# Starting a weight quantisation earlier and spacing it differently, beside a cross-attention on one core

## The chip, the cores and the metric

The kernel runs as one program on one core of a Trainium2 chip. The core has five instruction queues: PE (TensorE, matmuls), DVE (VectorE), ACT (ScalarE), POOL (GpSimd) and SP (SyncE, which here only issues transfers). Each queue runs its instructions in the order in which they were written; they meet through semaphores. The metric is the device time of one execution in microseconds (us).

## The reference, cut to what matters

A layer of a Perceiver-like network, in float32: 16 batches of 64 latents (1024 rows of width 512), each with a context of 512 rows of width 512.

```
x = x + cross_attention(latents = layernorm(x), context)    # 16 batches, 8 heads of 64
x = x + differential_self_attention(layernorm(x))            # rope, two softmaxes, rms norm
x = x + fp4_feed_forward(layernorm(x))

def cross_attention(latents, context):        # per batch
    kv = concat(norm(context), norm(latents)) @ w_kv          # keys and values, 512 + 64 rows
    out = softmax(q @ k.T) @ v
    return norm(out @ w_out) * g_o + b_o

def fp4_quant_dequant(w):                      # blocks of 16 along the last dimension
    scale = max(max(|block|) / 6, 1e-12)
    return grid_round(w / scale) * scale       # to 0, 0.5, 1, 1.5, 2, 3, 4, 6 with the sign

def fp4_feed_forward(x):                       # w_gate, w_up: 1408 x 512, w_down: 512 x 1408
    h = silu(q(x) @ q(w_gate).T) * (q(x) @ q(w_up).T)
    return q(h) @ q(w_down).T
```

The three weights of the feed-forward part are quantised on the chip, too. That work depends on nothing but the weights.

## The kernel before

Every float32 product is made of three products of rounded float32 (fp32r) halves: high by high, high by low, low by high. "High" is a copy into fp32r (on ACT), "low" the difference (on DVE or POOL). A product of 128 x 512 with a contraction of 512 is 12 matmuls.

The program has four stages: the latents' queries, keys and values (`latents`); the cross-attention, a loop over the 16 context batches (`cross_attention`, L1199); the self-attention over 8 tiles of 128 latent rows (`att.rest`); the feed-forward part (`ff.rest`). Up to the end of the self-attention each engine runs in the order in which the Python code writes its instructions (`in_order`, L87); so where a helper is called in the loop decides what it stands behind on every engine.

One context batch `b` of the loop, as PE sees it: four key products (`keys`, PSUM tile `pk`), the scores of the first two head groups (`scores(b, 0)`, `sim`), the weighting with the probabilities of the batch before (`finish(b - 1)`, `av`), the scores of the second two (`scores(b, 1)`), then four value products (`values`, `pv`) with the transpose of the latents' probabilities (`turn_latents`, `prlt`) after the second of them. The product tiles share three PSUM buffers (`ps_mm`), the scores two (`ps_sim`). DVE scales the keys (L953, `k<-pk,row`), makes the masked minimum of the softmax (L1000, `least`), takes context statistics (L329, L330) and half of the low halves of the next context (L376, `x<-raw,x`; the other half is POOL's). ACT makes the exponentials (L1004), scales the values (L966), copies the high halves (L370) and splits and joins the probabilities for a transposing transfer (`halves` L1040, `join` L1060).

Every second batch finishes a tile `p` of 128 latent rows. For it, odd batches from 3 on (`done` is set) hold the output product as well: `out_turn`, `out_low`, `out_product(p)` (PSUM tile `po`), then `out_norm(p)` (L1155: DVE writes `oz`), then `out_add(p)` (L1161: three passes on POOL, the last of which adds to `x`). The next even batch takes the moments of the new `x` (`out_moments`, `st_a` on DVE at L150, then POOL).

Into this loop the quantisation of the feed-forward weights is laced. `Quantise` holds 35 jobs, pieces of 128 x 512 or 128 x 384. The loop calls `tick()` at up to ten places per batch, the steps; at a step each active piece advances by one yield, and every fourth step starts a new piece. A piece takes ten steps: a load issued by POOL (L287, `qw`), two steps on a reduce group on DVE (L199 to L203), then POOL's multiply with the reciprocal (L205), then a mask on DVE (L208) and a Relu on ACT (L211), two steps later two DVE passes (L213, L214), POOL's multiply with the scale (L216), DVE's 32 x 32 transpose (L296) and ACT's high copy (L297) into `qhl`, and DVE's subtraction (L299) with a store to DRAM issued by POOL (L301). `qw` has three buffers, `qe` and `qhl` one each. In batch 0 the step at the end of the loop body is the only one; batch 1 has eight, the others ten. POOL also makes the low halves of the output weight (`weight_o`, L135, `wol`) at the end of batch 0.

`moments` (L145) makes a tile's mean and 1/sqrt(var + eps) with two DVE instructions and two small POOL ones; `shift` (L162) adds a third POOL one, the negative product of the two, so that `shifted` (L169) can normalise with one ACT instruction.

Of the kernel before, what the change touches and what calls it, by code (L numbers as in the profile page):

```python
# [9 lines left out]
F32 = mybir.dt.float32  # L10
# [10 lines left out]
P = 128  # L21
# [225 lines left out]
class Quantise:  # L247
# [3 lines left out]

    EVERY = 4

    def __init__(self, cm, sc, i):
        self.cm, self.sc = cm, sc
        self.jobs = []
        for c, (at, n) in enumerate(CHUNKS):
            for w, name in (("g", "w_gate"), ("u", "w_up")):  # L260
                self.jobs += [(w, c, k, i[name][k * P : (k + 1) * P, at : at + n]) for k in range(KC)]
        for c, (at, n) in enumerate(CHUNKS):
            self.jobs += [
                ("d", c, k, i["w_down"][at + k * P : at + (k + 1) * P, :]) for k in range(n // P)
            ]
        self.jobs.reverse()
        self.clock, self.active = 0, []

    def home(self, w1, w2):
        self.w1, self.w2 = w1, w2  # L270

    def tick(self, new=True):

        if new and self.jobs and self.clock % self.EVERY == 0:
            self.active.append(self.piece(*self.jobs.pop()))
        self.clock += 1
        self.active = [job for job in self.active if next(job, None)]

    def finish(self, all=False):
# [589 lines left out]
def cross_attention(tc, cm, sc, i, cw, cx, w1, w2, att, quant):  # L869
# [21 lines left out]
    def columns_of(r):  # L891

        first = S * (1 - r)
        return slice(first, first + N + S), slice(S - first, S - first + N)

    state = {}
# [25 lines left out]
    def mask(b):  # L922
        if b < B:
            nc.scalar.activation(
                masks[b % 2][:, S : S + N], state[b]["mu"], AF.Identity, bias=cm.masked, scale=MASKED
            )
# [17 lines left out]
    def keys(b, m):  # L944

        k = ends[b, m // 2][:, m % 2, :]
        hi, lo = cx.done[b]
        cols = slice(m * P, (m + 1) * P)
        ps = cm.mm(f"pk_{b}_{m}")
        cm.product(  # L950
            ps, lambda c: (w_k[0][:, c, cols], w_k[1][:, c, cols], hi[:, c, :], lo[:, c, :]), range(KC)
        )
        nc.vector.tensor_tensor(k[:, S : S + N], ps, cx.row[b], ALU.mult)  # L953
        state[b]["k"].append(k)
# [14 lines left out]
    def scores(b, a):  # L969

        st = state[b]
        st["sim", a] = pss = [cm.two(f"sim_{b}_{a}_{r}") for r in range(2)]
        for h in range(2):
            for r in range(2):
                rows = slice(r * S, (r + 1) * S)
                at = columns_of(r)[0].start + h * half
                for c in range(2):
                    m = 2 * a + c
                    nc.tensor.matmul(  # L979
                        pss[r][c * S : (c + 1) * S, h, :half],  # L980
                        lhsT=queries[b % 2][rows, m, :],
                        rhs=st["k"][m][rows, at : at + half],
                        start=True,
                        stop=True,
                    )

    def softmax(b, a):
        st = state[b]
        both = w1.tile([P, 2 * (N + S)], F32, tag="pr", bufs=2, name=f"pr_{b}_{a}")
        st["whole", a] = both  # L990
        st["pr", a] = both.rearrange("p (r n) -> p r n", r=2)

        def two(t):
            return t.rearrange("p (h n) -> p h n", h=2)

        for r, ps in enumerate(st.pop(("sim", a))):
            mask = masks[b % 2][:, columns_of(r)[0]]
            pr = st["pr", a][:, r, :]
            least = cm.small.tile([P, 1], F32, tag="least", name=f"least_{b}_{a}_{r}")
            nc.vector.tensor_tensor_reduce(  # L1000
                two(pr), ps[:, :, :half], two(mask), -1.0, BIG, ALU.add, ALU.min, least
            )
            t = 2 * a + r
            nc.scalar.activation(  # L1004
                pr, pr, AF.Exp, bias=least, scale=-1.0, accum_out=st["tot"][:, t : t + 1]
            )
# [121 lines left out]
    def out_turn(p):  # L1128
        o = state.pop(("o", p))
        pt = cm.tr(f"ot_{p}")  # L1130
        cm.transpose_chunks(pt, o.rearrange("p a c r d -> p (a c r d)"), KC)
        oh = w1.tile([P, KC, P], F32R, tag="oh", name=f"oh_{p}")
        ol = w2.tile([P, KC, P], F32R, tag="ol", name=f"ol_{p}")
        for k in range(KC):
            src, bias = pt[:, k * P : (k + 1) * P], cw.bv[:, k : k + 1]
            nc.scalar.activation(oh[:, k, :], src, AF.Identity, bias=bias)
        state["oT", p] = oh, ol, pt
# [9 lines left out]
    def out_product(p):  # L1147
        oh, ol, _ = state.pop(("oT", p))
        po = cm.mm(f"po_{p}")
        cm.product(  # L1150
            po, lambda k: (oh[:, k, :], ol[:, k, :], w_o[0][:, k, :], w_o[1][:, k, :]), range(KC)
        )
        state["po", p] = po, cm.moments(po, f"o_{p}")

    def out_norm(p):  # L1155
        po, mv = state.pop(("po", p))
        z = w2.tile([P, D], F32, tag="one", name=f"oz_{p}")
        cm.normalize(z, po, f"o_{p}", mv)
        state["oz", p] = z

    def out_add(p):  # L1161
# [5 lines left out]
    def out_moments(p):  # L1167
        cm.shift(cm.x[p], f"a_{p}", cm.x_mv[:, p, :])
# [29 lines left out]
    cx.load(2)  # L1198
    for b in range(B):  # L1199

        def tick():
            if b:
                quant.tick()

        done = (b - 3) // 2 if b >= 3 and b % 2 else None
        last = b == B - 1
        keys(b, 0)
        if b:
            cx.load(b + 2)
        if last:  # L1210
            att.load("Wq")
            att.load("Wk")
        cx.high(b + 1, 0)
        if b >= 4 and b % 2 == 0:
            out_moments((b - 4) // 2)
        if b > 1:
            tick()
        if done is not None:
            out_turn(done)
        keys(b, 1)  # L1220
        cx.low(b + 1, 0)
        cx.high(b + 1, 1)
        if b:
            join(b - 1, 0)
        if b > 1:
            tick()
        keys(b, 2)
        if b:
            mask(b)
        if done is not None:  # L1230
            out_low(done)
        cx.fetch(b + 2, 0)
        if b == 0:
            for k in range(KC):
                load_o(k)
        cx.flat(b + 1)
        cx.low(b + 1, 1)
        cx.high(b + 1, 2)
        if b:
            join(b - 1, 1)  # L1240
        tick()
        if last:
            att.split("Wq", 0, 1)
        if b == 0:
            scores(b, 0)
            softmax(b, 0)
        keys(b, 3)
        cx.fetch(b + 2, 1)
        if b:
            scores(b, 0)  # L1250
            softmax(b, 0)
        cx.low(b + 1, 2)
        cx.high(b + 1, 3)
        if b:
            finish(b - 1)
            scores(b, 1)
            softmax(b, 1)
            around(b + 1, 1)
            around(b + 2, 0)
        tick()  # L1260
        values(b, 0)
        if b and not last:
            halves(b, 0)
        cx.every(b + 1)
        cx.low(b + 1, 3)
        cx.stats(b + 2, 0)
        tick()
        if last:
            att.split("Wq", 2, 3)
            att.load("Wv")  # L1270
        if b == 0:
            scores(b, 1)
            softmax(b, 1)
            around(b + 1, 1)
            around(b + 2, 0)
        values(b, 1)
        if b == 0:
            halves(b, 0)
        if not last:
            turn_latents(b)  # L1280
            halves(b, 1)
            send(b, 0)
        begin(b + 1)
        latents_values(b + 1)
        cx.fetch(b + 2, 2)
        cx.stats(b + 2, 1)
        tick()
        if last:
            att.norm(0)
            att.split("Wk", 0, 1)  # L1290
        tick()
        if done is not None:
            out_product(done)
        tick()
        values(b, 2)
        if not last:
            send(b, 1)
        cx.fetch(b + 2, 3)
        cx.stats(b + 2, 2)
        tick()  # L1300
        if done is not None:
            out_norm(done)
            out_add(done)
        if b == 0:
            weight_o(0)
            weight_o(1)
        if b == 5:
            att.sa.work()
        if last:
            att.split("Wk", 2, 3)  # L1310
            att.load("Wo")
            att.turn(0)
        values(b, 3)
        cx.stats(b + 2, 3)
        cx.spread(b + 2)
        if b == 0:
            weight_o(2)
            weight_o(3)
        quant.tick()
# [693 lines left out]
```

## Time and profile before

| | |
|---|---|
| median of 3 runs | 876.33 us (874.78 to 876.99) |
| the profiled execution | 878.15 us, span 876.4 us |
| busy in the span: PE, DVE, ACT, POOL | 98%, 79%, 56%, 39% |
| transfers | 126.79 MB, mean 145 GB/s |
| first key product of batch 0, last of batch 15 | 81.6 us, 529 us |
| mean granted TensorE clock | 0.996 of full speed |

All times of a view count from the start of the span. "Busy" is time in which an engine's datapath ran; matmuls are pipelined, so a row for several of them shows the stretch that they span. In a list of waits, `A <- B` says that engine A sat idle before an instruction until B had ended; the numbers are the total, the count and the longest. In the order of time a bracket at the end of a row gives the idle time before it and what ended it. In a table of stretches, the columns are the stretch, its length, the busy time of each engine with the number of instructions, the granted clock, the share of the 16 DMA engines and the rate.

### The profile page before, as it was taken

How to read it: one execution, taken by the hardware profiler on the slowest of the kernel's cores; microseconds unless marked ns; L12 is line 12 of the kernel's file. 1: busy time of each engine (PE TensorE's matmuls, PEld its weight loads, DVE VectorE, ACT ScalarE, POOL GpSimd, SP SyncE). 2: the span in 40 equal slices, each digit the busy share in tenths (PEclk: the TensorE clock that was granted, in tenths of full speed). 3: DMA queues.
4: the chain of work that ended last, by engine and by line, in shares of the span. 5: the costliest groups of instructions: out<-in, count | busy, mean ns of one | idle time of the engine just before them, and what ended most of it. 6: DMA issues, size and time to landing. Idle time of an engine off the chain costs nothing.

```text
span 876.4 us, 16721 instructions
## 1 busy us (share of the span) xinstructions
PE 859.5 (98%) x6263; PEld 706.9 (81%) x6263; DVE 690.3 (79%) x1457; ACT 486.4 (56%) x847; POOL 345.6 (39%) x413
## 2 busy tenths in 40 slices
PE   9999999999999999999999999999999999999998
PEld 8988777887887777778877877878888888888886
DVE  7734457988789877887897776698998898888876
ACT  5654675766758757667767576544556232332221
POOL 3334144546465474364654733555543120111100
PEclk9999999999999999999999999999999999999999
DMA  7664767775975777668857564150008330000000
GB/s 243 207 229 170 198 183 202 207 190 182 235 186 154 216 211 202 168 177 224 192 148 211 159 162 182 49 193 2 2 1 336 121 144 24 1 13 13 13 13 24
DMA packets 135607, 126.79 MB, mean 145 GB/s; under 512 B 95512, under 2 KB 98472, under 8 KB 134248
## 3 DMA queue, kind: packets, MB, share of 16 engines
q1 hardware_dynamic: 127912, 99.26, 39.2%
q0 software_dynamic: 7616, 26.48, 9.3%
q8 instruction: 49, 0.80, 0.4%
q14 instruction: 30, 0.25, 0.1%
HBM read 84.26 MB, written 25.72 MB: 125 GB/s over the span
## 4 chain that ended last, share of the span: by engine, by line
PE 84%; DVE 7%; POOL 3%; ACT 2%; DMA 2%; issue 1%; DVEq 0%; POOLq 0%; ACTq 0%
PE pv L126 18%; PE pk L126 14%; PE gu L126 14%; PE dn L126 7%; PE sim L979 4%; PE av L1101 3%; PE Wv L126 3%; PE wo L126 3%; PE lv L126 2%; PE Wq L126 2%; PE Wk L126 2%; PE lq L126 2%; PE lk L126 2%; PE po L126 1%; PE ht L176 1%
## 5 line engine op out<-in xcount | busy, mean ns | idle before, releaser
L126 PE MATMUL pv<-xvh,x 128*128 128x512 f32 x512 | 136.9, 399 | 0.3 <-ACT v L966 0.3
L126 PE MATMUL pk<-x,xkh 128*128 128x512 f32 x512 | 127.2, 390 | 0.0
L126 PEld LDWEIGHTS pv<-xvh,x 128*128 128x128 f32 x512 | 95.2, 190 | 26.8 <-issue 7.3
L126 PEld LDWEIGHTS pk<-x,xkh 128*128 128x128 f32 x512 | 95.5, 188 | 19.8 <-issue 0.4
L1004 ACT ACTIVATE pr<-pr,least 128x576 f32<-128x576 f32 x64 | 49.1, 769 | 60.0 <-DVE least L1000 60.0
L953 DVE TENSOR_TENSOR k<-pk,row 128x512 f32<-128x512 f32 x64 | 42.9, 671 | 39.1 <-PE pk L126 31.6
L126 PE MATMUL pv<-xvl,x 128*128 128x512 f32 x256 | 70.0, 396 | 0.0
L126 PE MATMUL pk<-x,xkl 128*128 128x512 f32 x256 | 68.5, 389 | 0.0
L1060 ACT COPY prT<-far 128x1024 uint16<-128x1024 uint16 x60 | 67.3, 1173 | 1.3 <-DMA far<-half 1.3
L126 PE MATMUL gu<-uT,fx 128*128 128x512 f32 (+1 forms) x288 | 66.8, 377 | 0.0
L966 ACT ACTIVATE v<-pv,rs 128x512 f32<-128x512 f32 x64 | 43.9, 685 | 41.1 <-PE pv L126 40.1
L126 PE MATMUL gu<-gT,fx 128*128 128x512 f32 (+1 forms) x288 | 65.8, 376 | 0.0
L376 POOL TENSOR_TENSOR x<-raw,x 128x512 fp32r<-128x512 f32 x32 | 41.8, 1306 | 55.3 <-ACT x L370 47.4
L1040 ACT COPY half<-pr 128x1024 uint16<-128x1024 uint16 x60 | 59.8, 1048 | 0.0
L126 PEld LDWEIGHTS gu<-gT,fx 128*128 128x128 f32 x288 | 52.2, 188 | 7.6 <-ACT fx L134 0.2
L126 PEld LDWEIGHTS pv<-xvl,x 128*128 128x128 f32 x256 | 49.1, 192 | 11.0
L126 PEld LDWEIGHTS gu<-uT,fx 128*128 128x128 f32 x288 | 51.9, 188 | 7.2
L126 PEld LDWEIGHTS pk<-x,xkl 128*128 128x128 f32 x256 | 48.1, 188 | 10.0
L979 PE MATMUL sim<-k,mask 64*64 64x288 f32 x512 | 43.8, 418 | 9.3 <-DVE least L1000 7.9
L1000 DVE CUSTOM_DVE_ANT_0 pr<-sim,mask 128x576 f32<-128x576 f32 x64 | 45.8, 753 | 5.7 <-PE sim L979 2.8
L211 ACT ACTIVATE qe_h<-qe_h,mmagic 128x512 f32<-128x512 f32 (+1 forms) x24 | 16.5, 688 | 59.1 <-DVE qe_h L208 56.9
L126 PE MATMUL dn<-dT,hh 128*128 128x512 f32 x170 | 42.9, 392 | 0.0
(357 smaller groups left out, 1942.1 us busy)
## 6 DMA issues: line engine op xcount, KB each, us to landing
nat<-in_ctx_dram SPq DMA_DIRECT2D x16, 1024.0 KB
raw<-in_ctxT_dram SPq DMA_DIRECT2D x64, 256.0 KB
d_d<-qhl_d POOLq DMA_DIRECT2D x11, 512.0 KB, 3.8
row<-rs_d SPq DMA_DIRECT2D x16, 256.0 KB
g_d<-qhl_g POOLq DMA_DIRECT2D x8, 512.0 KB, 4.4
u_d<-qhl_u POOLq DMA_DIRECT2D x8, 512.0 KB, 4.6
gT<-g_d SPq DMA_DIRECT2D x4, 1024.0 KB
uT<-u_d SPq DMA_DIRECT2D x4, 1024.0 KB
```

The source lines that it names most:

```text
L126: self.nc.tensor.matmul(ps, lhsT=p[i], rhs=p[j], start=start and n == 0, stop=stop and n == last)
L176: self.nc.tensor.transpose(pt[:, c * P : (c + 1) * P], src[:, c * P : (c + 1) * P], self.ident)
L211: nc.scalar.activation(e, e, AF.Relu, bias=self.mmagic, scale=MAGIC)
L376: by.tensor_tensor(lo, self.raw[:, c, :], f32(hi), ALU.subtract)
L953: nc.vector.tensor_tensor(k[:, S : S + N], ps, cx.row[b], ALU.mult)
L966: nc.scalar.mul(v, ps, cx.rs[b][:, t : t + 1])
L979: nc.tensor.matmul(pss[r][c * S : (c + 1) * S, h, :half], lhsT=queries[b % 2][rows, m, :], rhs=st["k"][m][rows, at : at + half], start=Tru ...
L1000: nc.vector.tensor_tensor_reduce(two(pr), ps[:, :, :half], two(mask), -1.0, BIG, ALU.add, ALU.min, least)
L1004: nc.scalar.activation(pr, pr, AF.Exp, bias=least, scale=-1.0, accum_out=st["tot"][:, t : t + 1])
L1040: nc.scalar.copy(half, src[:, h])
L1060: nc.scalar.copy(dst, src)
L1101: nc.tensor.matmul(st["av"][r][rows, a, :], lhsT=prT[:, j, rows], rhs=st["v"][j][:, at : at + S], start=False, stop=j == NJ - 1, skip_grou ...
```

## The change

The step runs in batch 0 too, at the eight places where the loop body reaches it there, and at ten places in batch 1. Instead of one piece per four steps, one starts per three steps in batches 0 and 1, then per four in even batches and per five in odd ones; the first starts at the first step. The moments of the output product get the third POOL instruction, and `out_norm` becomes one ACT instruction instead of one DVE instruction. In batch 0 the first scores come after the fourth key product and not before it, as in all other batches.

```diff
-    EVERY = 4
-
     def __init__(self, cm, sc, i):
...
-        self.clock, self.active = 0, []
+        self.every, self.since, self.active = 3, 2, []
...
     def tick(self, new=True):
 
-        if new and self.jobs and self.clock % self.EVERY == 0:
+        self.since += 1
+        if new and self.jobs and self.since >= self.every:
             self.active.append(self.piece(*self.jobs.pop()))
-        self.clock += 1
+            self.since = 0
         self.active = [job for job in self.active if next(job, None)]
...
-        state["po", p] = po, cm.moments(po, f"o_{p}")
+        mv = cm.small.tile([P, 3], F32, tag="mv3", name=f"mv_o_{p}")
+        cm.shift(po, f"o_{p}", mv)
+        state["po", p] = po, mv
 
     def out_norm(p):
         po, mv = state.pop(("po", p))
         z = w2.tile([P, D], F32, tag="one", name=f"oz_{p}")
-        cm.normalize(z, po, f"o_{p}", mv)
+        cm.shifted(z, po, mv)
         state["oz", p] = z
...
     for b in range(B):
 
-        def tick():
-            if b:
-                quant.tick()
-
+        tick = quant.tick
+        quant.every = 3 if b < 2 else 4 + b % 2
...
             out_moments((b - 4) // 2)
-        if b > 1:
+        if b:
             tick()
         if done is not None:
             out_turn(done)
...
             join(b - 1, 0)
-        if b > 1:
+        if b:
             tick()
         keys(b, 2)
...
-        if b == 0:
-            scores(b, 0)
-            softmax(b, 0)
         keys(b, 3)
         cx.fetch(b + 2, 1)
-        if b:
-            scores(b, 0)
-            softmax(b, 0)
+        scores(b, 0)
+        softmax(b, 0)
         cx.low(b + 1, 2)
         cx.high(b + 1, 3)
```

## The prediction

> **What bounds the kernel now.** I read the page's busy line, then the list of PE's waits, then a table of stretches, one for each context batch (each begins with the batch's first key product), and then the order of time of DVE and POOL around the stalls found.
>
> ```profile
> PE 859.5 (98%) x6263; PEld 706.9 (81%) x6263; DVE 690.3 (79%) x1457; ACT 486.4 (56%) x847; POOL 345.6 (39%) x413
> ```
> ```profile
> PE sim L979 <- DVE least L1000: 7.9, 6, 1.6
> PE sim L979 <- DMA mask<-q_d: 1.4, 1, 1.4
> ```
> ```profile
> core 0: us, PE busy (x) PEld busy (x) DVE busy (x) ACT busy (x) POOL busy (x), PEclk, DMA share, GB/s
> 81.60:108.20 26.60, 25.22 (x132) 19.34 (x131) 10.50 (x23) 12.82 (x23) 5.18 (x8) 1.00 0.68 196
> 108.20:135.00 26.80, 26.80 (x212) 21.53 (x211) 13.96 (x32) 19.39 (x31) 11.66 (x13) 1.00 0.69 177
> 135.00:164.00 29.00, 27.43 (x211) 21.66 (x210) 24.07 (x54) 20.14 (x32) 13.55 (x16) 1.00 0.69 186
> ...
> 194.00:224.50 30.50, 29.04 (x212) 22.59 (x210) 26.66 (x58) 20.41 (x32) 19.13 (x23) 0.94 0.65 181
> 224.50:254.50 30.00, 30.00 (x228) 24.20 (x227) 23.61 (x53) 20.49 (x34) 13.48 (x16) 1.00 0.79 211
> ...
> 371.30:398.80 27.50, 27.50 (x212) 21.70 (x211) 23.61 (x56) 19.56 (x32) 16.52 (x22) 1.00 0.67 179
> ```
> PE is the bound, and only what makes it wait can be won. Odd batches from 3 on (224.5 to 254.5 is batch 5) carry the output product and lose nothing. Even batches hold 27.5 us of work, as batch 10 shows (371.3), but last 29.0, 30.5, 28.5, 28.4, 30.6 and 28.9 us as batches 2, 4, 6, 8, 12, 14. Batch 0 loses 1.4 us to the query load. In batches 4 and 12 the granted clock is 0.94: 0.06 of 30.5 us is 1.8 us lost at half rate, so a window of some 3.5 us ran at half clock right after the stall.
>
> Why even batches wait, seen in batch 4, DVE first and then POOL:
>
> ```profile
> 194.81 0.78 DVE L160 TENSOR_SCALAR oz<-po,mv_o 128x512 f32<-128x512 f32 x1
> 199.90 0.69 DVE L150 BATCH_NORM_STATS2 st_a<-x 128x6 f32<-128x512 f32 x1 [1.97 <-POOL x L1165]
> 205.21 2.08 DVE L201 SCALAR_TENSOR_TENSOR qs_u<-qm_u,least 128x32 f32<-128x32 f32 x1
> 209.06 0.75 DVE L1000 CUSTOM_DVE_ANT_0 pr<-sim,mask 128x576 f32<-128x576 f32 x1
> ```
> ```profile
> 195.67 1.29 POOL L1163 TENSOR_TENSOR oz<-oz,g_o 128x512 f32<-128x512 f32 x1 [0.41 <-DVE oz L160]
> 198.57 1.29 POOL L1165 TENSOR_TENSOR x<-x,oz 128x512 f32<-128x512 f32 x1
> ```
> Scores of the first half end at 205.7 on PE, their softmax pass starts at 209.06: DVE is 3.4 us late. PE covers about 1.9 us of that with the previous batch's weighting (batch 10 is 1.9 late and loses nothing); the rest is the wait.
>
> **The change, part by part.** Times are of the profiled run (span 876.4, 878.15 us in all); I forecast its difference and put that on the median, 876.33.
>
> *Fewer pieces in even batches, normalisation on ScalarE: a gain.* A piece costs DVE a reduce group of four instructions (0.7 + 0.2 to 2.1 + 0.2 + 0.35), an exponent mask (0.3 to 0.4), two scalar-tensor-tensors (0.7 each), a transpose (0.7) and a subtraction (0.65): about 4 us. Before, 2.5 pieces start per batch; now 9 in four batches, 2.25. From the output product's moments to the even batch's first softmax DVE had 14.5 us of work in its queue (summed from those rows); the changed kernel's order leaves 11.7 in batches 4, 8, 12 and 11.0 in 6, 10, 14. The normalisation (0.78) leaves DVE for ACT, which is idle 1.7 and 2.0 us around it (before the value scalings at 191.5 and 194.2). There it costs about 0.69, as ACT's PSUM read of the same size (L966), and can run when POOL has the variance: POOL's power ends at 192.4, one more small POOL operation (0.3 to 0.45, from L165) makes it 192.9, so the result stands at 193.6 instead of 195.6. POOL's three passes (1.3 + 1.45 + 1.3) follow in batches 6, 10, 14 at once, x is ready about 2 us sooner, and the 1.97 us wait shrinks to nothing; in 4, 8, 12 a multiply and a store go in between, and 1 us is gained. Lateness falls from 3.4 to 0.6 to 1.2 us, under the 1.9 that PE covers. Won: 3.0 + 1.0 + 0.9 + 3.1 + 1.4 (batches 4, 6, 8, 12, 14 against 27.5) = 9.4, less 0.3 should a slow L201 (2.08 above) recur: **-9.1** (bounds -7.5 and -9.7). Odd batches now have up to 8.4 us of DVE work before their softmax, against 6.7, with 10.9 us of key products to hide it: nothing. If ACT's wait on POOL ran long, the value scaling behind it would be late, which PE feels only at the third key product of the next batch, 8 us on: nothing. The last normalisation, after the batches, feeds a sum on POOL 16 us later: nothing.
>
> *Batch 0.* The last key product (12 matmuls, 2.7 us) now precedes the first scores and hides the query load: -1.4. But three pieces start here. POOL issues the first load behind its subtraction of 92.1, at 93.4, into the busiest stretch:
>
> ```profile
> 94.00:100.00 6.00, 6.00 (x39) 4.28 (x38) 3.12 (x7) 2.42 (x6) 1.28 (x1) 1.00 1.01 378
> ```
> Weight loads land 2.7 to 7.5 us after issue; the two that POOL issued at 82.9 and 83.7 took 5.8 and 6.8, nearest in place, so I take 5.8: 99.2. DVE's reduce for it stands in front of the second softmax, which ran at 99.74: 99.2 + 1.9 (reduce group) + 1.4 (softmax) + 0.9 (ACT's exponential) = 103.4. PE's transpose of the latents needs that and would be due at 102.5 - 1.4 = 101.1: 2.3 lost, net **+0.9** (+2.6 if landed in 7.5; -0.3 if in 2.7, since the statistics in front of the reduce hold it until about 98.0).
>
> *Batch 1.* DVE's transpose of the first piece now stands between the first and second key scalings and waits for POOL's second multiply. That is queued behind the four subtractions of the output weight:
>
> ```profile
> 108.60 2.55 POOL L135 TENSOR_TENSOR wol<-raw_wo,woh 128x512 fp32r<-128x512 f32 x2 [11.51 <-ACT woh L134]
> 112.78 2.54 POOL L135 TENSOR_TENSOR wol<-raw_wo,woh 128x512 fp32r<-128x512 f32 x2
> 115.27 0.62 POOL L287 DMA_DIRECT2D qw_g<-in_w_gate_dram  x1
> ```
> ACT gets from 103.4 to the first high half in 5.9 (as before) + 0.6 (a piece's Relu): 109.9. POOL needs 6.7 from there to the end of the four and 1.05 for the multiply: 117.6. Behind the transpose DVE has 8.9 us until its first softmax is through (transpose 0.6, reduce 1.9, three scalings 1.8, x 0.85, subtraction 0.6, two passes 1.3, small ones 0.4, softmax 1.4): 126.5. PE's second scores, at 122.53 before and now due at 123.4, wait **+3.1** (bounds 1.5 and 4.5, by slack in POOL). ACT's transposed probabilities, behind the same piece's copy, come at about 125 and are covered by this.
>
> *Batch 2.* Between batch 1's last softmax and batch 2's first key scaling DVE has three transposes, three reduce groups, four statistics, two subtractions, two pairs, two masks: 15.2 us, while PE gives it 11.9. Each transpose also waits for the previous store out of the single q_hl buffer (stores land after 2.8 to 8.3, median 4.0) and each reduce for its load: about 3.7 by that median. It comes 7 us late; two products (5.4) hide part, and the batch's own head, again with a store to wait for, adds 2.4: 4.0 of stalls against 1.5 now, **+2.5** (bounds -1 and +5).
>
> *Clock.* Of the seven stalls of 0.9 to 1.6 us two were followed by a half-rate window. Three new or longer ones in batches 0 to 2: one window, **+1.6** (0 to 3.3).
>
> The Trainium skill, "TensorE: Matmul & The Clock Gate", section "Part 1: The HAM clock gate (the "warmup" mystery)", says that the clock falls only after an idle window of about 3.4 us. The two windows at 0.94 after stalls of 1.5 us speak against that here; by the rule this term would be 0 and the sum 1.6 lower.
>
> The skill's "DMA: Bandwidth & Descriptors", section "Queues, rings and completion order", has each DMA engine alternate between the rings with work, so that POOL's load would share with SyncE's and not queue behind them. By it the load of 93.4 would land at about 97 (an estimate: 0.5 MB at the 378 GB/s above, plus the shortest landing), and batch 0 would come out at -0.3. The 7.5 us landing, issued 1 us behind a 1 MB load, speaks for queueing.
>
> *Free.* The 35 loads and 35 stores are the same, only earlier; SyncE's order is unchanged, PE's but for the swap.
>
> Sum: -9.1 + 0.9 + 3.1 + 2.5 + 1.6 = **-1.0**: 877.1 for the profiled run, 875.3 on the median. Measurement can tell about 0.3% (2.6 us).
>
> **Rivals.** *The start is absorbed (faster).* The first load lands fast, POOL finds room before the output weight, stores land in 3 us: batch 0 at -0.3, batch 1 at +1.5, batch 2 at 0, no half-rate window: -7.9, 868; with a little of each term left, up to 872. For it: batches 0 and 1 have DVE busy for only 10.5 and 14.0 us of 26.7. Against: the waits are of order, not of load.
>
> *The start overruns (slower).* The single q_hl buffer paces pieces that come every third step: a store landing near 8 us in batch 1 puts DVE 11 us behind, batch 2 loses 6, two half-rate windows follow: 2.6 + 4.5 + 5 + 3.3 - 9.1 = +6, 882. It decides once batches 0 to 2 lose over 9 us together. For it: the row of 8.3 and DMA share 1.03 at 136 to 142.
>
> *The gain fails to come.* If the x sum still ends late, behind the store queued before it, half of the 9.1 stays: +4, 880.
>
> **How the numbers follow.** Forecast 0.42 (872.3 to 878.3; 0.08 of it below 873.7), absorbed 0.30, overruns 0.19, gain fails 0.09. Faster 0.38, same 0.34, slower 0.28. The range 870 to 881 cuts the ends of the first two rivals.
>
> **What would show it.** Right: even batches from 4 on at 27.5 us with clock 1.00; no wait of DVE on the x sum over 1.3 us; batches 0 to 2 together about 6.5 us longer than 82.4; waits of PE on the latents' transposes (batch 0) and of DVE's L296 on POOL's L216 (batch 1). Wrong: a start that grows by under 3 us, or waits on the softmax that remain in even batches.

## The result, and the profile after

The changed kernel takes 900.22 us (median of 5 runs, 899.43 to 902.28) against 876.33 of the kernel before (5 runs, 874.77 to 877.19): 1.028 times, 95% interval 1.026 to 1.030. The forecast was 875.3, range 870 to 881. The profiled execution after took 899.45 us, its span is 897.5: 21.1 us more than the span before. The page's busy line and the list of PE's waits, to be held against those in the prediction:

```profile
PE 866.3 (97%) x6263; PEld 710.3 (79%) x6263; DVE 680.7 (76%) x1449; ACT 491.8 (55%) x855; POOL 344.6 (38%) x421
```
```profile
PE av L1100 <- ACT prT L1059: 6.4, 8, 3.1
PE sim L978 <- DVE least L999: 5.6, 3, 3.1
PE av L1084 <- DVE k L952: 4.9, 3, 1.9
PE zt L176 <- ACT oz L171: 2.5, 1, 2.5
PE prlt L1069 <- ACT pr L1003: 2.1, 1, 2.1
```

Before, nearly all of PE's idle time stood behind the softmax (`least`). Now it waits for DVE's keys and for ACT's copies too. (Most lines are one lower than before: L1000 is now L999.) The table of stretches, each from a batch's first key product, shows where they lie: batches 0, 1, 2, 4 and 7. (The columns are those of the prediction's table.)

```profile
81.74:108.82 27.08, 24.96 (x131) 19.02 (x130) 12.83 (x31) 12.93 (x23) 8.45 (x12) 1.00 0.74 224
108.82:143.82 35.00, 30.60 (x211) 23.68 (x210) 28.12 (x54) 22.58 (x37) 17.76 (x20) 0.90 0.64 170
143.82:178.16 34.34, 29.86 (x212) 22.99 (x210) 29.59 (x53) 20.43 (x32) 14.74 (x18) 0.95 0.65 179
...
211.93:240.98 29.05, 27.70 (x211) 21.71 (x211) 21.54 (x48) 19.49 (x31) 16.74 (x21) 1.00 0.64 177
...
298.46:330.76 32.30, 30.89 (x228) 24.49 (x226) 24.53 (x62) 20.44 (x36) 14.69 (x19) 1.00 0.67 187
```

Batch 1 takes 35.0 us in place of 26.8 and batch 2 34.3 in place of 29.0, at a granted clock of 0.90 and 0.95. Batch 4 gains 1.5. Batch 7, an odd batch in which nothing was lost before, is 2.3 longer. The whole difference, from the first key product of each batch, in us:

| stretch | before | after | forecast of the difference | measured |
|---|---|---|---|---|
| batches 0 to 2 | 82.4 | 96.4 | +6.5, and +1.6 of clock | +14.0 |
| odd batches 3 to 13 | 179.8 | 189.8 | 0 | +10.0 |
| even batches 4 to 14 | 174.4 | 168.6 | -9.1 | -5.8 |
| behind the batches | 327.2 | 330.0 | 0 | +2.8 |

What DVE waits for shows a new kind. These three lines are from the list of DVE's waits; the reduce L199 is the first instruction of a piece behind its load. Before, the three summed to 10.7 us, now to 44:

```profile
DVE qm_g L199 <- DMA qw_g<-in_w_gate_dram: 21.0, 9, 4.2
DVE qm_d L199 <- DMA qw_d<-in_w_down_dram: 12.2, 6, 4.0
DVE qm_u L199 <- DMA qw_u<-in_w_up_dram: 10.8, 7, 5.6
```

In batch 4 that wait stands ahead of the output product's moments. The order of time on DVE there, which answers to the four rows shown of before:

```profile
207.69 0.69 DVE L199 TENSOR_REDUCE qm_g<-qw_g 128x32 f32<-128x512 f32 x1 [4.20 <-DMA qw_g<-in_w_gate_dram]
...
209.13 0.64 DVE L150 BATCH_NORM_STATS2 st_o<-po 128x6 f32<-128x512 f32 x1
...
218.83 0.70 DVE L150 BATCH_NORM_STATS2 st_a<-x 128x6 f32<-128x512 f32 x1 [3.15 <-POOL x L1166]
```

The reduce waits 4.2 us for its load, the moments of `po` stand behind it, so ACT can normalise only when batch 4 is 2 us old. `x` is ready 6.9 us after the batch's start (5.9 before), and DVE waits 3.15 us for it where it waited 1.97. In batches 8 and 12 the reduce at that place waits 2.9 us each. In batches 6, 10 and 14, where no reduce stands there, `x` is ready 3.0 to 3.5 us after the start (4.9 to 5.9 before).

In batch 1, DVE and then POOL:

```profile
117.78 0.71 DVE L295 STREAM_TRANSPOSE qhl_g<-qw_g 128x512 f32<-128x512 f32 x1 [5.34 <-POOL qw_g L216]
...
122.28 3.85 DVE L214 SCALAR_TENSOR_TENSOR qw_g<-qw_g,qe_g 128x512 f32<-128x512 f32 x1
...
128.06 0.74 DVE L999 CUSTOM_DVE_ANT_0 pr<-sim,mask 128x576 f32<-128x576 f32 x1
```
```profile
116.69 1.05 POOL L216 TENSOR_TENSOR qw_g<-qw_g,qs_g 128x512 f32<-128x512 f32 x1
...
122.64 1.12 POOL L205 TENSOR_TENSOR qw_g<-qw_g,qm_g 128x512 f32<-128x512 f32 x1
...
124.25 1.31 POOL L375 TENSOR_TENSOR x<-raw,x 128x512 fp32r<-128x512 f32 x1
```

The transpose waits for POOL's multiply as forecast, 117.78 against 117.6. New is the second row: L214, 0.69 us when alone, lasts 3.85, and ends 0.6 us behind the second of two POOL instructions on whole tiles (125.56). From the transpose to the end of the second softmax pass (129.5) DVE takes 11.7 us where the prediction summed 8.9; the 3.2 us by which this L214 is longer cover the difference of 2.8.

In batch 2 PE's longest wait is not for the softmax. ACT and then PE:

```profile
159.53 0.72 ACT L211 ACTIVATE qe_u<-qe_u,mmagic 128x512 f32<-128x512 f32 x1 [6.70 <-DVE qe_u L208]
```
```profile
162.49 0.69 PE L1100 MATMUL av<-v,prT 128*64 128x64 f32 x16 [3.07 <-ACT prT L1059]
```

The join of the probabilities (`prT`, L1059) is queued on ACT behind this Relu of a piece, and the Relu waits 6.7 us for DVE's mask, which is late.

In batch 3, which carries an output product, DVE's order of time holds this row:

```profile
190.64 0.69 DVE L199 TENSOR_REDUCE qm_g<-qw_g 128x32 f32<-128x512 f32 x1 [2.79 <-DMA qw_g<-in_w_gate_dram]
```

Two key scalings follow it, at 192.08 and 193.78, and PE waits 1.9 us for the first.

Behind the batches, ACT and then PE:

```profile
596.94 0.78 ACT L171 ACTIVATE oz<-po,mv_o 128x512 f32<-128x512 f32 x1 [3.24 <-POOL mv_o L165]
```
```profile
597.77 1.12 PE L176 MATMUL zt<-ident,z 128*128 128x128 f32 x4 [2.48 <-ACT oz L171]
```

The last normalisation waits on ACT for POOL, and the copies that free PE's next PSUM tile are queued behind it.

### The profile page after: what moved, and what is told of

Read it like the earlier page. It is cut to its first block, busy times and chain, and to the rows that moved or that the text cites. A ratio compares the mean times of both kernels' runs of the same rounds, so it can differ in the third digit from the quotient of the medians.

```text
span 897.5 us, 16699 instructions
## 1 busy us (share of the span) xinstructions
PE 866.3 (97%) x6263; PEld 710.3 (79%) x6263; DVE 680.7 (76%) x1449; ACT 491.8 (55%) x855; POOL 344.6 (38%) x421
## 4 chain that ended last, share of the span: by engine, by line
PE 59%; DVE 12%; DMA 11%; ACT 7%; issue 5%; POOL 4%; SPq 1%; DVEq 0%; ACTq 0%; POOLq 0%
PE gu L126 14%; PE pv L126 8%; PE dn L126 7%; PE pk L126 4%; PE Wq L126 3%; DMA qw_g<-in_w_gate_dram 3%; PE Wv L126 2%; PE wo L126 2%; PE Wk L126 2%; DMA qw_d<-in_w_down_dram 2%; PE sim L978 2%; PE av L1100 2%; PE lq L126 2%; PE lk L126 2%; ACT prT L1059 2%
## 5 line engine op out<-in xcount | busy, mean ns | idle before, releaser
L1059 ACT COPY prT<-far 128x1024 uint16<-128x1024 uint16 x60 | 67.3, 1172 | 0.0
L126 PEld LDWEIGHTS pv<-xvl,x 128*128 128x128 f32 x256 | 48.2, 188 | 10.7
L978 PE MATMUL sim<-k,mask 64*64 64x288 f32 x512 | 46.6, 434 | 6.0 <-DVE least L999 5.6
L999 DVE CUSTOM_DVE_ANT_0 pr<-sim,mask 128x576 f32<-128x576 f32 x64 | 45.7, 751 | 6.0 <-PE sim L978 1.9
L328 DVE BATCH_NORM_STATS2 cst<-nat 128x6 f32<-128x512 f32 x64 | 42.8, 669 | 1.3 <-DMA nat<-in_ctx_dram 1.3
```

Of the source, the lines that this page charges most:

```text
L126: self.nc.tensor.matmul(ps, lhsT=p[i], rhs=p[j], start=start and n == 0, stop=stop and n == last)
L328: nc.vector.bn_stats(st, self.nat[b][:, j, :])
L978: nc.tensor.matmul(pss[r][c * S : (c + 1) * S, h, :half], lhsT=queries[b % 2][rows, m, :], rhs=st["k"][m][rows, at : at + half], start=Tru ...
L999: nc.vector.tensor_tensor_reduce(two(pr), ps[:, :, :half], two(mask), -1.0, BIG, ALU.add, ALU.min, least)
L1059: nc.scalar.copy(dst, src)
```

## The experiments

The first four experiments take the change apart. Theory O: three separate losses of order (start, late loads in odd batches, the last normalisation). The rivals blame the normalisation itself (N), the steady rate (R), or a backlog that would come in any case (S).

**e1, only the normalisation moved.** Edit to the kernel before:

```diff
-        state["po", p] = po, cm.moments(po, f"o_{p}")
+        mv = cm.small.tile([P, 3], F32, tag="mv3", name=f"mv_o_{p}")
+        cm.shift(po, f"o_{p}", mv)
+        state["po", p] = po, mv
...
-        cm.normalize(z, po, f"o_{p}", mv)
+        cm.shifted(z, po, mv)
```

> The kernel before with nothing changed but the normalisation of the output product, moved to ACT. Theory O (the loss is one of order: 17.8 us at the start, some 6 us in odd batches from the new rate, 2.8 us behind the last normalisation): even batches from 4 on lose 1 us less each than before, some -4 in all, because DVE has 0.78 us less in front of the softmax and x is ready sooner; behind the batches the last normalisation waits on ACT for POOL and costs +2.5 to +4. Sum 875 to 877 against 876.3. Rival N (the normalisation itself does the harm: ACT waits for POOL in every pair of batches and all that is queued behind it on ACT is late): 882 or more, with PE waits on ACT's copies in even batches.

876.15 us (872.68 to 878.93), ratio 0.9987 (0.9971 to 1.0003). In its profile the even batches 4 to 14 take 168.1 us, 6.3 less than before, odd ones 179.8 as before, and the tail 330.2, 3.0 more. So the normalisation alone gives all of the even batches' gain that the changed kernel shows (5.8), and pays half of it back behind the batches. N falls for the steady part. The profiled execution of e1 is the fastest of its ten (872.68 us) and the only one at a granted clock of 1.000; in the others it is 0.994 to 0.998, so the median holds half-rate windows that this profile does not show. Two of PE's waits, the softmax in even batches and the new one:

```profile
PE sim L979 <- DVE least L1000: 5.1, 5, 1.2
PE zt L176 <- ACT oz L171: 2.5, 1, 2.5
```

**e2, the normalisation back on DVE** (the reverse of e1's edit, in the changed kernel).

> The changed kernel with the normalisation back on DVE, all else as changed. Theory O: the tail loses 2.8 to 4 us less, the even batches 2 to 4 more: 898 to 901 against 900.2 of the changed kernel. Rival N: most of the 24 us goes away, 890 or less.

890.3 us (888.23 to 894.39): 10 less than the changed kernel, far more than O's 2, and only just above N's bound. Its profiled execution is the longest of its runs (span 892.6), so the profile shows 4.9 of the 10: 3.3 in the tail, 2.3 in even batches. O expected the even batches to lose 2 to 4 us by this edit. They gained: 166.3 us, with all normalisations on DVE, against 168.6 in the changed kernel. In these two profiles the move to ACT wins nothing in the even batches once the rate is the new one. See e12.

**e3, the old start with the new rate.** The start of the kernel before (no step in batch 0 but the last, eight in batch 1, every fourth, old place of the scores), and:

```diff
-        quant.every = 3 if b < 2 else 4 + b % 2
+        quant.every = 4 + (b % 2 if 2 <= b < 10 else -1 if b == 14 else 0)
+        if b == 2:
+            quant.since = 2
```

> The changed kernel with the start of before: the one step in batch 0, eight in batch 1, a piece per four steps there, and the first scores of batch 0 in their old place. From batch 2 the same steps start pieces as in the changed kernel up to batch 8; from batch 10 on every fourth step, and every third in batch 14, so that all 35 are done. Theory O: batches 0 to 2 as long as before (82.4 us together), so the 14 us lost there go away; odd batches 3 and 7 still lose 2 to 4 us each on loads that land late: 880 to 885. Rival S (a queue that is fuller from the start on is only the first to show what the steady rate costs): batches 2 to 4 lose what 1 to 3 lost, 890 or more.

907.65 us, a miss for both: batch 15 took 51.3 us in place of 31.0, since my four pieces of batch 14 run on into the first self-attention work. That total says nothing. The batches ahead of it do: 0 to 2 take 84.5 us against 96.4, and batch 3 takes 37.7, with DVE waiting 5.0 us for one load and 4.9 for a store out of `qhl`. But `since = 2` lets the first piece of batch 2 start two steps behind the last of batch 1 (their loads are issued at 139.02 and 140.25), so batch 3 does not tell what the rate does without the new start; e10 does.

**e4, the new start with the old rate from batch 2 on.**

```diff
-        quant.every = 3 if b < 2 else 4 + b % 2
+        quant.every = 3 if b < 2 else 4
+        if b == 2:
+            quant.since = 0
```

> The changed kernel with its new start, but from batch 2 on a piece at every fourth step, at the very steps of before. Theory O: batches 0 to 2 keep the 14 us that they lost; the odd batches 3, 7 and 11 last 30 us again, even ones 28.5 to 29.5: 894 to 898. Rival R (the rate per four and five is what harms, the start has only a few us of its own): 885 or less.

890.99 us, ratio 1.0165 (1.0144 to 1.0186): 9 less than the changed kernel, below O's range and above R's. Odd batches 5 to 13 are back at 149.9 (156.0 after, 149.8 before), batches 0 to 2 still take 96.3. So the new rate costs 9 us here, the start some 15 (e4 against e1).

The next four ask why, and try the first better version.

**e5, the normalisation on ACT for all tiles but the last.** e1, with `if p < NT - 1:` around the ACT form, and the first scores of batch 0 behind the fourth key product.

> The kernel before with the normalisation on ACT for all tiles but the last, which stays on DVE, and with the first scores of batch 0 behind the fourth key product. No change to the pieces of quantisation. If the parts are what they seem (e1: some 6 us less in batches 4 to 14, 3 us more behind the batches): 872 to 874, the tail as long as before (327). If the 3 us of the tail are due to something else in e1: 875 to 877. Batch 0 ends at 24.7 to 25.2 us in place of 26.6 if its loss was the query load in front of the scores.

869.35 us (868.75 to 870.3), ratio 0.9916 (0.9897 to 0.9934): faster than both kernels. The tail is 326.8 us again, and PE's wait on `oz` is gone. Batch 0 takes 25.1 us. e1's batch 0, with the scores in their old place, took 24.7 in its profiled execution and 26.6 before, so that loss comes and goes; what the swap gives by itself was not measured.

**e6, the output weight's low halves on DVE** (`nc.gpsimd` becomes `nc.vector` in `weight_o`, in e4).

> e4 (new start, a piece per four steps at the steps of before from batch 2 on) with the low halves of the output weight made by DVE and not by POOL. Theory Q (queue: the first piece's multiply stands behind these four on POOL, and DVE's transpose waits 5.6 us for it): batch 1 goes from 35.4 to 29 or 30 us, one or both half-rate windows go, batch 2 shrinks by 2 or more: 881 to 886 against 891. Rival L (load: DVE is busy 28.6 us in batch 1, more than the 26.8 us of products, so it is late whatever it waits for, and gets 2.6 us more here): batch 1 stays above 33 us, 889 or more.

888.57 us. DVE's wait for POOL's multiply falls from 5.6 us (e4) to 1.3, and batch 1 takes 32.7 us (35.4 in e4), batch 2 34.8 (34.6). PE's wait for the softmax in batch 1 stays at 3.05 us (3.08 in e4). The wait for POOL that the prediction named was worth 2.7 us of a loss of 15, with one half-rate window less among them; L's bounds are nearer.

**e7, loads one step earlier** (the changed kernel from batch 2 on; all other steps of a piece stay where they were).

```diff
         nc.gpsimd.dma_start(w, src)
         yield True
+        if self.every > 3:
+            yield True
...
         quant.every = 3 if b < 2 else 4 + b % 2
+        if b == 2:
+            quant.since += 1
```

> The changed kernel; from batch 2 on each piece issues its load one step earlier, and all its other steps stand where they stood. Theory O (the odd batches wait because a reduce stands two steps behind a load that lands late): DVE's waits on these loads fall from 44 us to under 20, odd batches 3, 7 and 11 go from 32.3 to 33.8 us to about 30: 889 to 894 against 900.2. Rival P (it is DVE's order, so many instructions in front of the keys at these steps, not the landing): 897 or more.

887.14 us (884.84 to 889.22), 13 less than the changed kernel and below O's range. DVE's waits on loads, and the stretches of batches 4 and 7:

```profile
DVE qm_u L199 <- DMA qw_u<-in_w_up_dram: 8.1, 6, 2.7
DVE qm_g L199 <- DMA qw_g<-in_w_gate_dram: 3.8, 2, 2.9
DVE qm_d L199 <- DMA qw_d<-in_w_down_dram: 3.6, 3, 2.4
```
```profile
209.18:235.97 26.79, 26.79 (x211) 21.51 (x210) 21.79 (x47) 19.65 (x31) 15.94 (x20) 1.00 0.76 196
...
293.97:323.93 29.96, 29.96 (x227) 24.16 (x226) 25.71 (x63) 21.65 (x37) 14.34 (x21) 1.00 0.75 204
```

44 us of waits became 15.5; batch 4 fell from 29.05 to 26.79, with no PE idle time left, batch 7 from 32.3 to 29.96. Even batches 4 to 14 now take 163.3 us, 11.1 less than before: the gain that was forecast is there once the loads are in time.

**e8, a piece per four steps in batches 0 and 1, too** (`quant.every = 4` throughout, in e4).

> e4 with a piece per four steps in batches 0 and 1, too (five pieces there, not six, starting at the second step). Theory Q: the first transpose stands one step later, waits about 2.7 us less for POOL, and batches 1 and 2 lose 3 and 2 us less: 885 to 888 against 891. Rival L (loss in step with the number of pieces): 15 us of loss becomes 12.5: 888 to 890.

873.88 us (873.46 to 874.94), ratio 0.997 (0.9956 to 0.9983): 17 us less than e4, where the theories expected 1 to 6. Batches 0 to 2 take 80.7 us against 96.3. Five pieces at four steps cost next to nothing (e1, with the old start, takes 80.2), six at three steps cost 15 us. The second pass L214, by the view of that line from 100 to 175 us (durations in ns as shortest/median/longest), of the changed kernel and then of e8:

```profile
L214 DVE SCALAR_TENSOR_TENSOR qw_g<-qw_g,qe_g x4: 691/2014/3848, 109.3 to 144.1; 128x512 f32<-128x512 f32 x4
L214 DVE SCALAR_TENSOR_TENSOR qw_u<-qw_u,qe_u x2: 2045/2140/2235, 154.1 to 169.1; 128x512 f32<-128x512 f32 x2
```
```profile
L214 DVE SCALAR_TENSOR_TENSOR qw_g<-qw_g,qe_g x4: 692/693/693, 107.2 to 143.7; 128x512 f32<-128x512 f32 x4
L214 DVE SCALAR_TENSOR_TENSOR qw_u<-qw_u,qe_u x2: 691/692/693, 157.2 to 164.2; 128x512 f32<-128x512 f32 x2
```

With pieces three steps apart, a piece's two long DVE passes (sixth step behind its load) stand in the same step as POOL's multiply of the next piece (third step), and five of six L214 last 2.0 to 3.8 us. DVE's work in its own order from batch 1's first key scaling to batch 2's, summed from its rows, is 19.2 us before, 34.7 after, 24.3 in e8; PE's batch holds 26.8.

The next four: what the parts make together.

**e9, three repairs at once** (the changed kernel with e8's start, e7's early loads, e5's last normalisation).

```diff
-        quant.every = 3 if b < 2 else 4 + b % 2
+        quant.every = 4 + (b % 2 if 2 <= b < 12 else 0)
+        quant.early = b > 1
+        if b == 2:
+            quant.since += 1
```

> The changed kernel with three edits: a piece per four steps in batches 0 and 1 (e8), from batch 2 on each load one step earlier than its piece's other steps need (as in e7), the last normalisation on DVE (e5). The rate is per four and five up to batch 11, then per four, so that all 35 pieces are done in time. If the three causes are separate: start +1.5 us against e5, even batches 4 us shorter than in e5, tail as in e5: 864 to 868, below e5's 869.4. If the lower rate in odd batches is worth nothing even with the loads in time: 870 to 873.

869.86 us, ratio 0.9918 (0.9897 to 0.9939): as e5. Even batches take 165.2 us (168.1 in e5), but batch 15 takes 33.7 (31.0), as the later pieces reach into it. 30 us of loss are gone, and what the lower rate gains is given back at the end.

**e10, e8's start alone** (the changed kernel with e9's line for `quant.every`, nothing else).

> The changed kernel with a piece per four steps in batches 0 and 1, and per four and five up to batch 11, per four from there; loads where they stood, all normalisations on ACT. Theory O (late loads harm by themselves): the start's 15 us go, 2 to 4 us are still lost in several odd batches, DVE still waits 20 us or more for loads: 880 to 886. Rival K (loads land late only because the start left DVE and POOL behind): odd batches at 30, 877 or less.

879.98 us, at O's lower bound: batches 0 to 2 take 79.5 us, odd ones 5 to 13 154.8, and DVE waits 30.5 us for loads. The late loads harm without the start.

**e11, early loads in e5.**

> e5 (869.4 us) with each load one step earlier from batch 2 on, the other steps of a piece where they were in the kernel before. Theory: the reduce that stands in front of the output product's moments and of the first softmax no longer waits; even batches 4, 6, 12 and 14 shrink from 28.5 towards 27.5: 865 to 868. If those waits are DVE's own load and not the landing: 868.5 to 870.5.

870.95 us: no gain. Four of the six even batches from 4 on last 28.6 us or more, one of them (30.5) with half-rate windows. At the old rate the loads were not what the even batches waited for.

**e12, only the last normalisation back on DVE** (e5's `if`, in the changed kernel).

> The changed kernel with only the last normalisation, behind the batches, back on DVE. The tail falls from 330.0 to 326.8 us and nothing else moves: 896 to 898. If the 10 us that e2 won (all normalisations back) lie in this one, through half-rate windows that the stall sets off: 890 to 893.

894.61 us, between the two: 5.6 less than the changed kernel, of which the profile shows 3.3 in the tail. By medians the other normalisations cost e2's further 4 us. The two profiles have nearly the same span (892.6 in e2, 893.0 in e12): even batches take 171.4 us in e12 against 166.3, odd ones 185.2 against 190.0. So where the 4 us lie is open; that the even batches are no shorter with the normalisation on ACT is what e2 showed, too.

After the first twelve, the cause of the start's 15 us was open: number of pieces, or their spacing.

**e13, no overlap of L214 and POOL's multiply** (in e6; one step less between a piece's Relu and its DVE passes while the rate is three).

```diff
-            if step == "relu":
+            if step == "relu" and self.every > 3:
```

> e6 (888.6 us: new start, low halves of the output weight on DVE, a piece per four steps from batch 2 on) with one step fewer between a piece's Relu and its two DVE passes while the rate is three, so that they no longer stand in the step of the next piece's multiply on POOL. Theory V (overlap with POOL stretches DVE): the second pass lasts 0.7 us in place of 2.0 to 3.8, DVE's work from batch 1's first key scaling to batch 2's falls from 34.7 to about 30 us, batches 1 and 2 lose 5 to 8 us less: 880 to 884. Rival L (the number of pieces): 887 or more.

885.14 us, 3.4 less than e6 and between the theories. L214 is at 0.69 us but once, and batch 1 falls from 32.7 to 28.5 us; but batch 2 stays at 34.2, with other waits (PE 2.6 us on ACT's value scaling, 1.8 on its probabilities, and a half-rate window), and batch 0 grows by 2.3, with a wait of 2.1 us and a window of its own. The sum of DVE's work in batch 1 is 33.7 us, not 30: steps moved forward bring other pieces' work with them.

**e14, one input for the small DVE instructions** (in e5).

```diff
-        nc.vector.scalar_tensor_tensor(s, m, 1.0 / 6.0, least, ALU.mult, ALU.max)
+        nc.vector.tensor_scalar(s, m, 1.0 / 6.0, 1e-12, ALU.mult, ALU.max)
-        nc.vector.scalar_tensor_tensor(m, s, 1.0 + SHADE, none, ALU.mult, ALU.max)
+        nc.vector.tensor_scalar(m, s, 1.0 + SHADE, 0.0, ALU.mult, ALU.max)
```

> e5 (869.4 us) with the two small DVE instructions of the reduce group that read two tiles (L201, L202, of which the second tile is a constant) written with two immediate numbers, so that they read one tile each. Theory V, if it takes two inputs from SBUF for a DVE instruction to be held up by POOL: the long L201 of 1.3 to 2.1 us, one in each of batches 4, 6, 8, 10, 12 and 14, goes to 0.2 to 0.6, the first softmax of the even batches is 1 to 1.5 us less late, and they last 27.5 and not 28.5: 865 to 867. If any DVE instruction is held up: no change, 868.5 to 870.5.

868.32 us (868.17 to 870.25), ratio 0.9915 (0.9897 to 0.9933): not to be told from e5. One of the three groups of L201 in the loop:

```profile
L201 DVE TENSOR_SCALAR qs_d<-qm_d x11: 182/616/2080, 394.6 to 511.7; 128x32 f32<-128x32 f32 x11
```

With one tile read it is held up just as long beside POOL.

**e15 and e16, the spacing of three in one batch only** (e4; e15 without steps in batch 0 but the last, e16 with `quant.every = 4 if b else 3`).

> e4 (891 us) with no step in batch 0 but the last, so that a piece per three steps begins only there and three times in batch 1: four pieces by the end of batch 1, against six in e4 and five in e8. Theory D (the spacing of three harms): batches 1 and 2 together take 59 us or more (56.0 in e8, 70.0 in e4), 876 to 882. Rival L (the number of pieces): 57 us or less, 872 to 875.

> e4 with a piece per three steps in batch 0 only and per four from batch 1 on: three pieces begin in batch 0 and two in batch 1, five in all as in e8. Theory D: batch 1 keeps the wait for POOL and one stretched pass, 30 to 33 us, batch 2 is near 28 to 30: 877 to 883. Rival L: as e8, 873 to 876.

883.17 us (ratio 1.0068, 1.0045 to 1.009) and 881.66 (1.0059, 1.0037 to 1.0081). Batches 1 and 2 together take 60.2 and 60.5 us, 56.0 in e8. Four pieces, fewer than e8's five, lose 9 us against e8 by the median when three steps lie between them, and five lose 8. It is not the number that costs but where the pieces stand, and the runs that lose are those with a spacing of three. Two things are not separated here. With the spacing the places in the loop change at which a piece's steps fall. And in e16 the first piece starts at the first step, in e8 at the second: batch 0 takes 29.0 us in e16 and 24.7 in e8, which is 4.3 us more, so part of e16's loss may be that. In e15 batch 0 is as in e8. L214 lasted 2.0 and 3.3 us in e15, 3.3 in e16. Which share is the stretching and which the waits that follow it is not separated: e13 removed most of the stretching and got 4.2 us in batch 1, and 3.4 in all.

## Why the prediction was wrong, point by point

The profiled run was forecast 1.0 us shorter and came 21.1 us longer. Of those 22 us the odd batches, put at nothing, are 10.0, batches 0 to 2 5.9, the even batches 3.3 and the last normalisation 2.8.

**Even batches, -9.1 forecast, -5.8 measured.** The failed step is "in 4, 8, 12 a multiply and a store go in between, and 1 us is gained": there a reduce stands in front of `po`'s moments and waited 4.2, 2.9 and 2.9 us for its load, so `x` was ready 6.9, 5.2 and 6.6 us after the batch's start (5.9, 5.7 and 5.9 before), not 1 us sooner. The cost of a piece included its four reduce instructions and not the wait in front of them. The step for 6, 10 and 14 held (`x` about 2 us sooner). With the loads in time (e7) the gain is 11.1. The two halves of this step, fewer pieces and the normalisation on ACT, do not add up as the prediction had it: the second alone gives 6.3 us (e1), the changed kernel without it 8.1 (e2), both together 5.8, each from one profile.

**"Odd batches ... nothing": +10.0.** This step failed outright. It compared busy time (8.4 us of DVE work against 10.9 of products), and DVE's order holds waits: in batches 3, 7 and 11 a reduce two steps behind a load waited 2.79, 2.78 and 2.47 us, in front of two key scalings. That load is issued late, behind POOL's chain for the row statistics, and within 1 us of a store: at 183.18 and 303.92 the loads landed after 7.44 and 6.72 us, at 220.50 and 293.10 after 2.94 and 2.82. The prediction listed these landings (2.7 to 7.5) and used them for batches 0 to 2 only. "The 35 loads and 35 stores are the same, only earlier" costed them at nothing; e7 shows that one step earlier for the loads is worth 13 us: 8.1 in odd batches, 5.3 in even ones.

**Batch 0, +0.9 forecast, +0.5 measured.** The forecast wait came: the load issued at 92.79 landed after 6.49 us (5.8 forecast), and PE waited 2.1 us for the latents' transposes (2.3 forecast). That the sum is so near is partly luck. The 1.4 us that the swap was to win are a wait that e1 did not have with the scores in their old place (24.7 us), and batch 0 of the same start took 26.1 us in e7's profile and 28.6 in e12's. The landing at about 97 that the prediction estimated by the Trainium skill ("DMA: Bandwidth & Descriptors", section "Queues, rings and completion order") did not come: 99.28.

**Batch 1, +3.1 forecast, +8.2 measured.** The waits named came: 5.3 us for POOL, then the softmax late. PE's idle time is 4.4 us, inside the bounds of 1.5 to 4.5: 1.3 for ACT's joined probabilities, then 3.08 for the softmax. Two sizes were wrong: DVE's 8.9 us were 11.7 through one stretched L214, and 6.83 us at half rate began in the stall, so that PE's busy time is 3.8 us longer, too (30.60 against 26.80). And the wait for POOL was not what mattered most: with it cut to 1.3 us (e6) PE waited as long for the softmax (3.05), and 2.7 us came back. The term that failed is DVE's work, summed from the rows of pieces spaced four steps, where L214 took 0.7.

**Batch 2, +2.5 forecast, +5.3 measured**, just over the bound of 5, and by another path. PE's waits, 4.5 us, are near the 4.0 forecast, but that is luck: the forecast had them behind DVE's keys, where 1.0 us lies, and 3.45 stand behind ACT's joined probabilities, which the prediction did not name in this batch. In e2, e4, e6, e7 and e12, which have the same six pieces, the longest of these waits is 2.9 to 3.1 us; in e8 it is not there. In front of batch 2's first key scaling DVE waited 0.5 and 1.9 us for loads and not for a store, less than the 3.7 assumed; two stretched passes, 1.3 us longer each, were not in the sum.

**"The last normalisation ... nothing": +2.8.** I followed its result to POOL's sum 16 us later, and not what is queued behind it on ACT: the copies that PE waits for. e1 and e5 settle it, 330.2 against 326.8, and e12 puts the last one alone back in the changed kernel: 326.7.

**Clock, +1.6 forecast.** Three windows of 3.41 us fell in batches 1 and 2, where one was forecast. They cost PE an estimated 4 us, since 2.2 us of the first lie in a stall; a fourth came behind the batches. The windows of batches 4 and 12 went, as forecast.

The rival "the start overruns" had the right direction and size for batches 0 to 2 (its terms make 15.4, 14.0 was lost), though its store out of `qhl` did not come; it priced the rest of the kernel at the full gain, and so ended at 882.

## What to carry to other kernels

A moved piece of work costs its waits as well as its instructions: for each load in the changed order, take the distance to its first reader and the longest landing seen, not the median, and ask what stands behind that reader. When work is interleaved by steps, write down which stages of neighbouring pieces share a step: here a spacing of three steps, which puts a long DVE pass beside a long POOL pass, cost some 15 us, and one of four next to nothing; how much of it is that overlap is not shown (with the overlap taken out, e13 won 3.4). And when an instruction changes engines, read the queue behind it on the new engine, the last time it runs included: leaving that one where it was won 5.6 us in the changed kernel (e12), and with the swap in batch 0 it made a version of 869.4 us (e5) out of one of 876.2 (e1).

## What the hardware did that was not expected

A DVE instruction can last as long as its neighbour on POOL. L214 took 0.69 us alone, 2.0 beside one POOL instruction of 1.1 us (at 136.75), 3.85 beside two, and ended 0.6 us behind the last of them; the small L201 takes 0.2 alone and up to 2.1. The Trainium skill, "SBUF — State Buffer", section "SBUF: two separate sides", names a port pair that DVE and GpSimd share as an exclusive lock, held for a whole instruction, with the loser blocked. The rows agree that DVE waits rather than shares. They don't show its rule that the one that starts first holds the pair: by the records, POOL's L205 began 0.37 us after L214, and L214 still outlasted it. e14 shows that two inputs are not needed for it, which the page's other case, an instruction in a two-port mode, would allow; no run here shows in which mode it ran.

The clock again fell after short stalls. The last normalisation on ACT leaves the same stall of PE, 2.48 us, in the profiles of eleven kernels (the changed one, e1, e3, e4, e6, e7, e8, e10, e13, e15 and e16). In eight of them a half-rate window of 3.41 or 6.83 us begins within 1.6 us of its end, in e1, e7 and e16 none. The rule of an idle window of some 3.4 us from the Trainium skill, "TensorE: Matmul & The Clock Gate" (section "Part 1: The HAM clock gate (the "warmup" mystery)") agrees with these three and not with the eight. In e5's profile, whose stalls in the batches are 1.1 us at most, no window follows any.
